# Picking the last tiles of every step by matmul, a third one in each fifth step, with the edge bias written into PSUM by ScalarE

## The chip, the core and the metric

The kernel runs on one core of a Trainium2 chip. The metric is the device time of one execution, in microseconds. An execution was also recorded by the hardware profiler; all instruction times below come from that record, and line numbers (L402) are lines of the kernel before.

## What is computed

A graph layer on 6250 nodes of 64 numbers and 206250 edges, sorted by destination. Of each edge, the key and value of its source node are needed, the query of its destination, and the edge's own projected features:

```
Qh, Kh, Vh = x @ Wq.T + bq, x @ Wk.T + bk, x @ Wv.T + bv     # (6250, 4 heads, 16)
Ee    = edge_attr @ We.T + be                                # (206250, 4, 16)
score = exp(clip((Kh[src] * Qh[dst] / 4 * Ee).sum(-1), -5, 5))
wV    = segment_sum(Vh[src] * score, dst)                    # (6250, 64)
out   = layernorm(x + wV)
```

## The kernel before

Edges are cut into 1612 tiles of 128, eight tiles to a group, and the loop at L708 goes through them in 105 steps: 97 of two groups (16 tiles) and 8 of one group at the end. What is written here is one branch of an If (L412); the other branch, a general method, is not taken by these inputs.

**Ahead of the loop.** Keys and values of all nodes are computed (L320, L322) and written to a table in HBM, kv_tab; the queries, split into three bf16 parts, to another, q3_tab. The kv of the first four groups are not taken from the table: GpSimd gathers rows of x (L230), and PE turns them and multiplies them by the weights (L370 to L384). GpSimd then gathers kv of groups 4 to 7 (L406).

**Keys and values of an edge (kv).** A ring of five buffers (KVB, L118) holds the kv of five steps, 16 tiles each. There are three ways into it. Nearly all tiles are gathered from kv_tab by one indirect DMA of GpSimd for each tile (gather_kv, L402). In every sixth step one tile comes row by row through SP's queue (fetch_rows, L528, and a copy, L548). And the last two tiles of most steps are "picked" by matmul: the nodes' x, in three bf16 parts, lies in SBUF as a table of 50 blocks of 128 rows (parts); VectorE compares the sources with the block numbers and makes a matrix of ones and zeros (hots, L481, in two halves of 25 blocks for each tile); 25 matmuls (a burst, L491) for each half pick the rows of x out of the table into PSUM; VectorE adds the three parts (picked, L498); PE turns the result (picked_turned, L505) and multiplies it by the weights (picked_kv, L513 and L515); ScalarE copies it into the ring (L516). A pick begun in step s delivers tiles 14 and 15 of step s + 2. In the kernel before, this is done in steps 4 to 94. The table is made in steps 0 to 3 by table_parts (L444): a load of x on SP's queue, copies by ScalarE and subtractions by VectorE.

**A step.** VectorE multiplies kv by the queries (products, L602) and by the edge values (L603), adds up each head (L609), clips it (L611); ScalarE takes Exp (L612); VectorE multiplies the values by it (message, L619). ScalarE and PE split the message into three bf16 parts (L622, and minus: L630, L632, twice). In the next step, 16 matmuls add up the messages by destination (sums, L638), and VectorE adds that to the open blocks of the output (add, L652). About every second step a block of 128 nodes is closed (close, L668, L677, L678); after 16, 32 and 47 closed blocks their norms follow, three in a step (norm, L688).

For the next step, while this one runs: PE spreads row numbers into PSUM (spread, L555), ScalarE makes of them a matrix of ones and zeros in two passes, Square (L572) and Relu (L577), PE multiplies the queries by it (queries, L595). PE also computes the next step's edge values in PSUM (edges, and edge_values L386): first a matmul that writes the bias (L388), then four f32 matmuls on top (L391), for each of the two groups.

**What sets the order.** The schedule is by hand: the order of the calls in the loop (L708 to L786) is the order in each engine's queue, and each engine goes through its queue in order. GpSimd's gathers of step s + 4 are called in step s, behind the message (L742); they write the ring buffer that step s - 1 has read. The PSUM tile pb is single, and spread and picked_turned take it in turn; so is pe, which the edge values of the next step overwrite when L603 has read them; and rows3, which the first burst of a step overwrites when L498 has read the picks of the step before. The tile small, also in PSUM, holds the turned sources, the scores and the sums side by side.

Of the kernel before, what the change touches and what calls it, by code (L numbers as in the profile page):

```python
# [14 lines left out]
P = 128  # L15
N = 6250
# [24 lines left out]
TB = 8  # L41
M0 = 4
# [21 lines left out]
LAST = NS - 8 - 3  # L64


def picks_in(s):
    return M0 <= s <= LAST

# [5 lines left out]
COLUMN = 2 * G - 3  # L75
# [27 lines left out]
def tile_gnn(ctx: ExitStack, tc: tile.TileContext, x, xT, wT, bias, beT, weT, eT, src, dst, dst_rows,  # L103
# [52 lines left out]
    bkv_p = consts.tile([3, G // 2, 2 * C], BF16, name="bkv_p")  # L156
    minus_b = consts.tile([P, P], BF16, name="minus_b")
# [26 lines left out]
    with tc.tile_pool(name="nodes", bufs=1) as nodes, \  # L184
# [36 lines left out]
        nc.sync.dma_start(be_sb, beT.to_broadcast([3, C]))  # L221
        nc.vector.memset(we_sb, 0.0)
# [147 lines left out]
        for g in range(XG):  # L370
            for h in range(2):
                tp = npsum.tile([P, 2, P], F32, name="tp", bufs=2)
                for u in range(2):
                    j = 4 * h + 2 * u
                    nc.tensor.transpose(tp[:, u, :],
                                        XS[g][:, j:j + 2, :].rearrange("p j c -> p (j c)"), ident)
                xe = nodes.tile([P, 2, P], F32, name="xe", bufs=2)
                nc.scalar.activation(xe, tp, AF.Copy)
                pv = npsum.tile([P, 4, 2 * C], F32, name="pv", bufs=2)
                nc.tensor.matmul(pv, ones_b, bkv_p, start=True, stop=False, skip_group_check=True)  # L380
                for u in range(2):
                    nc.tensor.matmul(pv[:, 2 * u:2 * u + 2, :], xe[:, u, :], wkv, start=False,
                                     stop=u == 1, skip_group_check=True)
                nc.scalar.activation(kv_of(g)[:, 4 * h:4 * h + 4, :], pv, AF.Copy)  # L384

    def edge_values(pe, et, n):  # L386

        nc.tensor.matmul(pe[:, :n, :], ones_b, be_p[:, :n, :], start=True, stop=False,  # L388
                         skip_group_check=True)
        for u in range(n // 2):  # L390
            nc.tensor.matmul(pe[:, 2 * u:2 * u + 2, :], et[:, u, :], we_sb, start=False,  # L391
                             stop=u == n // 2 - 1, skip_group_check=True)
# [13 lines left out]
    for g in range(XG, 2 * KVB - 2):  # L406
        for j in range(G):
            gather_kv(g, j)
# [3 lines left out]
    with tc.If(rv == 0) as branch:  # L412

        with tc.tile_pool(name="work", bufs=2) as work, \
# [5 lines left out]
            col, from0, from1 = (small[:, i * C:(i + 1) * C].bitcast(BF16) for i in range(3))  # L420
            from_b = from0, from1
            score_all = small[:, 3 * C:3 * C + 2 * G * H]
            pa = small[:, 4 * C:7 * C].rearrange("p (i c) -> p i c", i=3)
            nc.tensor.transpose(col, row_b[:, 0:1].to_broadcast([P, P]), ident_b)

            parts = accp.tile([P, NB, 3, C], BF16, name="parts")
            nc.vector.memset(parts, 0.0)
            NX = N // NB
            x_v = x.rearrange("(p b) c -> p b c", p=NX)
            n_picks = LAST - M0 + 1  # L430
            src_f = accp.tile([P, n_picks, 2], F32, name="src_f")
            t0 = (M0 + 3) * 2 * G - 2
            for i in range(2):
                nc.vector.tensor_copy(src_f[:, :, i],
                                      src_i[:, t0 + i:t0 + i + 2 * G * (n_picks - 1) + 1:2 * G])
            pick = fixed.tile([P, 4 * P], F32, name="pick")
            rows3 = pick[:, :6 * C].rearrange("p (k i c) -> p k i c", k=2, i=3)
            HOT, FAR, X = {}, {}, {}
# [5 lines left out]
            def table_parts(b):  # L444

                n = min(TB, NB - b)
                raw = work.tile([P, TB, C], F32, name="raw", bufs=1)
                nc.sync.dma_start(raw[:NX, :n], x_v[:, b:b + n, :])
                rest = pick[:NX, :n * C].rearrange("p (b c) -> p b c", b=n)
                nc.scalar.activation(rest, raw[:NX, :n], AF.Copy)  # L450
                nc.scalar.activation(parts[:NX, b:b + n, 0], raw[:NX, :n], AF.Copy)
                return rest

            def table_parts_rest(b, rest):
                n = min(TB, NB - b)
                nc.vector.tensor_sub(rest, rest, parts[:NX, b:b + n, 0])
                nc.scalar.activation(parts[:NX, b:b + n, 1], rest, AF.Copy)
                nc.vector.tensor_sub(parts[:NX, b:b + n, 2], rest, parts[:NX, b:b + n, 1])

            def sources(s, i):  # L460

                if picks_in(s):
                    FAR[s, i] = work.tile([P, P], BF16, name="far")
                    nc.scalar.activation(FAR[s, i], row50, AF.Identity,
                                         bias=src_f[:, s - M0, i:i + 1], scale=-1.0)

            def sources_turned(s, i):
                if picks_in(s):  # L470
                    nc.tensor.transpose(from_b[i], FAR.pop((s, i)), ident_b)  # L471
# [4 lines left out]
            def hots(s, i, h):  # L476

                if picks_in(s):
                    HOT[s, i, h] = work.tile([P, NB // 2, P], BF16, name="hot", bufs=4)
# [6 lines left out]
            def picks(s, i, h):  # L486
                if picks_in(s):
                    hot = HOT.pop((s, i, h))
                    for k in range(NB // 2):
                        b = h * NB // 2 + k  # L490
                        nc.tensor.matmul(rows3[:, i], hot[:, k, :], parts[:, b], start=b == 0,  # L491
                                         stop=b == NB - 1)

            def picked(s):

                if picks_in(s):
                    xp = work.tile([P, 2, C], F32, name="xp")
                    nc.vector.tensor_reduce(xp, rows3.rearrange("p k i c -> p k c i"), axis=AX.X,  # L498
                                            op=OP.add)
                    X[s] = xp  # L500

            def picked_turned(s):
                if picks_in(s):
                    room = psum.tile([P, G, P], F32, name="pb")
                    nc.tensor.transpose(room[:, 0, :], X[s].rearrange("p k c -> p (k c)"), ident)  # L505
                    xe = work.tile([P, P], F32, name="xe")
                    nc.scalar.activation(xe, room[:, 0, :], AF.Copy)
                    X[s] = xe, room[:, 4:6, :]

            def picked_kv(s):  # L510
                if picks_in(s):
                    xe, kv = X.pop(s)
                    nc.tensor.matmul(kv, ones_b, bkv_p[:, :2], start=True, stop=False,  # L513
                                     skip_group_check=True)
                    nc.tensor.matmul(kv, xe, wkv, start=False, stop=True, skip_group_check=True)  # L515
                    nc.scalar.activation(kvs[(s + 2) % KVB][:, 2 * G - 2:, :], kv, AF.Copy)  # L516

            def gather(s):
                for g in groups_of(s):
                    for j in range(tiles_of(g)):  # L520
                        if is_rowed(s) and (g - STEPS[s][0]) * G + j == COLUMN:
                            continue
                        if not picks_in(s - 2) or g == STEPS[s][0] or j < G - 2:
# [36 lines left out]
            def edges(s, k):  # L560

                g = STEPS[s][0] + k
                if k == 0:
                    PE[s] = psum.tile([P, 2 * G, C], F32, name="pe")
                edge_values(PE[s][:, k * G:(k + 1) * G], ET[g], tiles_of(g))
# [134 lines left out]
            closed, scaled, normed = 0, 0, 0  # L700
            keys(0)
# [5 lines left out]
            onehot_edges(0)  # L707
            for s in range(NS):  # L708
# [9 lines left out]
                if more:  # L718
                    onehot_rows(nexts[0], spread(nexts[0]))
                    onehot_rows_rest(nexts[0])  # L720
# [4 lines left out]
                if nexts[1:]:  # L725
                    onehot_rows(nexts[1], spread(nexts[1]))
                making = [b for b in range(s * 2 * TB, (s + 1) * 2 * TB, TB) if b < NB]
                if making:
                    rest = table_parts(making[0])
                prod = products(s)  # L730
                picked(s - 1)
                if more:
                    edges(s + 1, 0)
                picks(s, 0, 0)
                score = scores(s, prod)
                if nexts[1:]:
                    onehot_rows_rest(nexts[1])
# [5 lines left out]
                picked_turned(s - 1)  # L743
                if nexts[1:]:
                    edges(s + 1, 1)
                minus(s, msg, 0)
                hots(s, 1, 0)
                picks(s, 0, 1)
                minus(s, msg, 1)
                picked_kv(s - 1)  # L750
# [5 lines left out]
                picks(s, 1, 0)  # L756
                sources(s + 1, 1)
                sources(s + 2, 0)
                if s + 1 < NS:
                    rows_fetched(s + 1)  # L760
                if more:
# [5 lines left out]
                hots(s + 1, 0, 0)  # L767
                hots(s + 1, 0, 1)
# [14 lines left out]
                for i, b in enumerate(making):  # L783
                    if i:
                        rest = table_parts(b)
                    table_parts_rest(b, rest)  # L786
# [4 lines left out]
            scales(B - 2, B - 1)  # L791
            norm(B - 2)
            last_add(NS - 1)
            spreads(B - 1)
            roots(B - 1, B)
            scales(B - 1, B)
            norm(B - 1)

    with branch.Else():

        sums = [dram.tile([NR, C], F32, name=f"sums{i}") for i in range(TABLES)]
        with tc.tile_pool(name="gconsts", bufs=1) as gc, \
                tc.tile_pool(name="gloads", bufs=3) as loads, \
                tc.tile_pool(name="ggath", bufs=4) as gath, \
# [28 lines left out]
            def gather(g, j):  # L833
# [3 lines left out]
                if g >= 2 * KVB - 2:  # L837
# [11 lines left out]
            def compute(g):  # L849
# [33 lines left out]
                AGG[g] = work.tile([P, G, C], F32, name="agg", bufs=3)  # L883
# [79 lines left out]
```

## Time and profile before

| | |
|---|---|
| time, median of 3 runs | 1790.06 us (1789.95 to 1790.13) |
| the profiled execution's own time | 1789.88 us |
| its span, first to last instruction | 1788.0 us |
| PE, TensorE's matmuls, busy | 1638.5 us (92%) |
| PEld, its weight loads, busy | 1369.6 us (77%) |
| DVE, VectorE, busy | 1481.6 us (83%) |
| ACT, ScalarE, busy | 914.0 us (51%) |
| POOL, GpSimd, busy | 1337.4 us (75%) |
| matmuls that pick (L491) | 9100, 828.3 us |
| granted TensorE clock, mean | 0.951 |

A line of the groups gives the source line, engine, operation, what it writes and reads with shapes and how many, then the busy time and the mean of one in ns, then how long the engine was idle just before them and what ended that. In a timeline the first two columns are the start and the duration in us. Matmuls are pipelined, so a busy PE isn't PE at its peak. "Issue" is time in which an engine waited for nothing that the profile shows. A line of the windows gives the stretch, its length, then PE, PEld, DVE, ACT and POOL busy with their counts, the granted clock, the share of DMA and GB/s.

### The profile page before, as it was taken

The numbers are of one execution on the slowest core, as the hardware profiler recorded it, in microseconds if no ns is written. First come the engines' busy times: TensorE is split into PE (matmuls) and PEld (weight loads), VectorE is DVE, ScalarE is ACT, GpSimd is POOL, SyncE is SP. The second block draws the span as 40 slices with busy tenths as digits, with TensorE's granted clock in tenths as the row PEclk, the third lists the DMA queues.
The fourth block names the chain that finished last, engine by engine and source line by source line (L and its number), as shares of the span: only waits on it lengthen the run. The fifth ranks groups of instructions, "written<-read, shape, count | busy, mean of one in ns | idle before, by whom it ended". The sixth has DMA issues, their size and how long they took to land.

```text
span 1788.0 us, 44286 instructions
## 1 busy us (share of the span) xinstructions
PE 1638.5 (92%) x15751; PEld 1369.6 (77%) x15751; DVE 1481.6 (83%) x1695; ACT 914.0 (51%) x1328; POOL 1337.4 (75%) x1427
## 2 busy tenths in 40 slices
PE   8978999999999998999999899999989998999864
PEld 8647888888888787787887778777877887787632
DVE  6459999999998898888889888888988888898654
ACT  3465555555554464454455445455544554455443
POOL 7777777777777777777777777777777777777774
PEclk9968999999999999999999999999999999999855
DMA  7443333333333333332333333323332333333331
GB/s 221 132 121 84 90 93 94 93 94 92 93 81 94 93 86 89 92 94 80 93 93 81 93 81 93 92 81 99 87 93 80 94 93 81 93 90 81 91 80 44
DMA packets 109970, 166.71 MB, mean 93 GB/s; under 512 B 69196, under 2 KB 71452, under 8 KB 109626
## 3 DMA queue, kind: packets, MB, share of 16 engines
q0 software_dynamic: 45280, 91.78, 19.4%
q1 hardware_dynamic: 64074, 71.01, 14.1%
q8 instruction: 125, 2.05, 0.5%
q10 hardware_dynamic: 384, 1.00, 0.3%
q14 instruction: 107, 0.88, 0.2%
HBM read 156.33 MB, written 7.33 MB: 92 GB/s over the span
## 4 chain that ended last, share of the span: by engine, by line
PE 38%; POOL 29%; issue 14%; DVE 13%; DMA 4%; ACT 3%; DVEq 0%; SPq 0%; POOLq 0%; ACTq 0%
POOL kv L402 29%; PE pick L491 18%; PE pe L391 5%; DVE hot L481 5%; DMA kv<-kv_tab,src_i 3%; PE pq L630 2%; PE small L638 2%; DVE prod L603 2%; DVE prod L602 2%; PE pb L555 2%; PE pe L388 2%; PE pb L515 1%; PE pq L595 1%; DVE pq L619 1%; PE ps L350 1%
## 5 line engine op out<-in xcount | busy, mean ns | idle before, releaser
L402 POOL DMA_INDIRECT kv<-kv_tab,src_i x1383 | 1305.3, 944 | 421.7 <-issue 399.8
L491 PE MATMUL pick<-parts,hot 128*128 128x192 bf16 x9100 | 828.3, 249 | 0.0
L491 PEld LDWEIGHTS <-hot 128*128 128x128 bf16 x9100 | 771.7, 99 | 38.1
L481 DVE TENSOR_TENSOR hot<-small,block 128x3200 bf16<-128x3200 bf16 x364 | 645.3, 1813 | 0.4 <-PE pick L491 0.4
L572 ACT ACTIVATE to<-pb,minus_row 126x1024 bf16<-126x1024 f32 x202 | 222.7, 1102 | 371.0 <-PE pb L555 367.2
L632 ACT ACTIVATE msg<-pq 128x1024 bf16<-128x1024 f32 (+2 forms) x210 | 207.6, 989 | 222.3 <-PE pq L630 222.3
L391 PEld LDWEIGHTS pe<-we_sb,et 128*128 128x128 f32 x1612 | 209.7, 203 | 133.4 <-issue 95.3
L602 DVE TENSOR_TENSOR prod<-kv,pq 128x1024 f32<-128x1024 f32 (+2 forms) x105 | 123.5, 1176 | 169.3 <-DMA kv<-kv_tab,src_i 52.0
L391 PE MATMUL pe<-we_sb,et 128*128 128x128 f32 x1612 | 250.3, 302 | 0.0
L577 ACT ACTIVATE to<-to,one_p 126x1024 bf16<-126x1024 bf16 x202 | 230.6, 1142 | 3.5
L638 PEld LDWEIGHTS <-of 128*128 128x128 bf16 x1612 | 145.3, 102 | 31.1 <-issue 7.9
L638 PE MATMUL small<-msg,of 128*128 128x192 bf16 x1612 | 161.9, 257 | 0.5 <-ACT msg L632 0.5
L388 PE MATMUL pe<-be_p,ones_b 3*128 3x512 bf16 x202 | 79.7, 395 | 86.3 <-DVE prod L603 86.1
L630 PE MATMUL pq<-msg,minus_b 128*128 128x512 bf16 x404 | 128.0, 396 | 33.1 <-ACT msg L622 19.5
L622 ACT ACTIVATE msg<-pq 128x1024 bf16<-128x1024 f32 (+2 forms) x105 | 103.8, 989 | 96.8 <-DVE pq L619 96.8
L609 DVE TENSOR_REDUCE small<-prod 128x64 f32<-128x1024 f32 (+2 forms) x105 | 123.6, 1177 | 14.5 <-PE small L471 8.8
L555 PE MATMUL pb<-key_rows,ident_b 112*128 112x512 bf16 x403 | 127.9, 400 | 2.8 <-ACT to L572 2.8
L603 DVE TENSOR_TENSOR prod<-prod,pe 128x1024 f32<-128x1024 f32 (+2 forms) x105 | 123.6, 1177 | 3.6
L619 DVE TENSOR_TENSOR pq<-kv,small 128x1024 f32<-128x1024 f32 (+2 forms) x105 | 123.4, 1175 | 1.4 <-ACT small L612 1.4
L585 DVE TENSOR_TENSOR of<-small,key 128x2048 bf16<-128x2048 bf16 (+2 forms) x105 | 122.9, 1171 | 0.3
L595 PEld LDWEIGHTS <-to 126*128 126x128 bf16 x1612 | 63.5, 101 | 25.3 <-issue 25.1
L612 ACT ACTIVATE small<-small 128x64 f32<-128x64 f32 (+2 forms) x105 | 21.7, 207 | 111.1 <-DVE small L611 109.2
(129 smaller groups left out, 996.4 us busy)
## 6 DMA issues: line engine op xcount, KB each, us to landing
et<-in_eT SPq DMA_DIRECT2D x100, 512.0 KB
rk<-kv_tab SPq DMA_DIRECT2D x1920, 0.5 KB
kv<-kv_tab,src_i POOLq DMA_INDIRECT x1383
qw<-q_tab SPq DMA_DIRECT2D x202, 15.8 KB
kv_tab<-kv_sb SPq DMA_DIRECT2D x5, 640.0 KB
q_tab<-q SPq DMA_DIRECT2D x5, 480.0 KB
acc<-in_x SPq DMA_DIRECT2D x48, 32.0 KB
out<-y SPq DMA_DIRECT2D x48, 32.0 KB
```

Of the source, the lines that this page charges most:

```text
L391: nc.tensor.matmul(pe[:, 2 * u:2 * u + 2, :], et[:, u, :], we_sb, start=False, stop=u == n // 2 - 1, skip_group_check=True)
L402: nc.gpsimd.indirect_dma_start(out=kv_of(g)[:, j, :], out_offset=None, in_=kv_tab[:, :], in_offset=bass.IndirectOffsetOnAxis(ap=src_i[:, t ...
L481: nc.vector.tensor_tensor(HOT[s, i, h].rearrange("p b (a c) -> p b a c", c=2), pairs(from_b[i])[:, None].to_broadcast(shape), block2[:, bl ...
L491: nc.tensor.matmul(rows3[:, i], hot[:, k, :], parts[:, b], start=b == 0, stop=b == NB - 1)
L555: nc.tensor.matmul(pb[:, b:b + 4, :], ident_b[:NR2, g // 2:g // 2 + 1].to_broadcast([NR2, P]), key_rows[:, g % 2, b * P:(b + 4) * P], star ...
L572: nc.scalar.activation(TO[g][:, :n, :], pb[:3 * W, :n, :], AF.Square, bias=minus_row3[:3 * W])
L577: nc.scalar.activation(TO[g][:, :n, :], TO[g][:, :n, :], AF.Relu, bias=one_p[:3 * W], scale=-1.0)
L602: nc.vector.tensor_mul(prod[:, :n, :], kvs[s % KVB][:, :n, :C], PQ[s][:, :n, :])
L603: nc.vector.tensor_mul(prod[:, :n, :], prod[:, :n, :], PE[s][:, :n, :])
L630: nc.tensor.matmul(msg[:, lo:hi, :], minus_b, M3[s][:, lo:hi, i, :], start=False, stop=True, skip_group_check=True)
L632: nc.scalar.activation(M3[s][:, :n, i + 1, :], msg[:, :n, :], AF.Copy)
L638: nc.tensor.matmul(PA[s], OH[s][:, j, :], M3[s][:, j], start=j == 0, stop=j == n - 1)
```

## The change

- Steps 0 to 96 pick (before: 4 to 94), and every fifth step from 0 to 90 picks a third tile, tile 13 of step s + 2. The tile that comes row by row moves from 13 to 12. The third tile's hots, its two bursts (into the PSUM tile pb) and one more reduction stand at the end of the step and at the head of the next; its x is turned and multiplied apart (64 rows). There are five hot tiles and three far tiles instead of four and two.
- The table of parts is made ahead of the loop, from the transposed x that already lies in SBUF: 50 transposes on PE, copies by ScalarE, subtractions by VectorE, placed between the kv of the first four groups, whose turning now goes one half ahead. The seven loads in steps 0 to 3 go, and a load of the bias for all partitions joins SP's queue at the start.
- The edge bias of steps 1 to 104 is written into PSUM by one ScalarE copy for a step (biases), and the edge matmuls add to it. pe is a fixed tile. Step 0 keeps its two bias matmuls.
- In a step the sums come first on PE; the first spreading comes behind the sources, and on ScalarE its Square and Relu stand around Exp and the bias; the second spreading and the edges of both groups come behind the first burst, the message and the gathers' call.
- picked_turned goes from ahead of the first subtraction to behind the second burst, picked_kv from there to behind the third burst.
- At the very end, the last addition goes ahead of scales and norm of the block before the last.

```diff
+THIRD = 5
+TB = 4
-LAST = NS - 8 - 3
+LAST = NS - 8 - 1
+def picks_third(s):
+    return picks_in(s) and s % THIRD == 0 and STEPS[s + 2][1] == 2
...
+            px = npsum.tile([P, 2, 2 * C], F32, name="ps").rearrange("p i (j c) -> p (i j) c", j=2)
+            px = px[:, :n]
+            for u in range(n):
+                nc.tensor.transpose(px[:, u, :], xT_sb[:C, (b + u) * P:(b + u + 1) * P],
+                                    ident[:C, :C])
+            nc.scalar.activation(parts[:, b:b + n, 0], px, AF.Copy)
+            nc.vector.tensor_sub(px, px, parts[:, b:b + n, 0])
+            halves.append((px, b, n))
...
+    def edge_values(pe, et, n, biased=False):
+
+        if not biased:
+            nc.tensor.matmul(pe[:, :n, :], ones_b, be_p[:, :n, :], start=True, stop=False,
+                             skip_group_check=True)
...
+                    if i == 2 and h == 0:
+                        R3[s] = psum.tile([P, G, P], F32, name="pb")
...
+            def picked_third(s):
+
+                if picks_third(s):
+                    to = R3.pop(s).rearrange("p g e -> p (g e)")[:, :3 * C]
+                    nc.vector.tensor_reduce(X[s][:, 0], to.rearrange("p (i c) -> p c i", i=3),
+                                            axis=AX.X, op=OP.add)
...
+            def biases(s):
+                n = tiles_in(s)
+                nc.scalar.activation(pe_all[:, :n, :], be_all[:, None, :].to_broadcast([P, n, C]),
+                                     AF.Copy)
...
                 nexts = list(groups_of(s + 1)) if more else []
-                if more:
-                    onehot_rows(nexts[0], spread(nexts[0]))
-                    onehot_rows_rest(nexts[0])
                 if s:
                     sums(s - 1)
                 sources_turned(s, 1)
                 sources_turned(s + 1, 0)
-                if nexts[1:]:
-                    onehot_rows(nexts[1], spread(nexts[1]))
-                making = [b for b in range(s * 2 * TB, (s + 1) * 2 * TB, TB) if b < NB]
-                if making:
-                    rest = table_parts(making[0])
+                sources_turned(s, 2)
                 prod = products(s)
                 picked(s - 1)
+                picked_third(s - 1)
                 if more:
-                    edges(s + 1, 0)
+                    onehot_rows(nexts[0], spread(nexts[0]))
                 picks(s, 0, 0)
                 score = scores(s, prod)
-                if nexts[1:]:
-                    onehot_rows_rest(nexts[1])
+                if more:
+                    biases(s + 1)
+                    onehot_rows_rest(nexts[0])
                 if s:
                     add(s - 1)
                 msg = message(s, score)
                 if s + KVB - 1 < NS:
                     gather(s + KVB - 1)
-                picked_turned(s - 1)
                 if nexts[1:]:
-                    edges(s + 1, 1)
+                    onehot_rows(nexts[1], spread(nexts[1]))
+                for k in range(len(nexts)):
+                    edges(s + 1, k)
                 minus(s, msg, 0)
+                if nexts[1:]:
+                    onehot_rows_rest(nexts[1])
                 hots(s, 1, 0)
                 picks(s, 0, 1)
+                picked_turned(s - 1)
                 minus(s, msg, 1)
-                picked_kv(s - 1)
...
                 hots(s, 1, 1)
                 picks(s, 1, 0)
+                picked_kv(s - 1)
                 sources(s + 1, 1)
                 sources(s + 2, 0)
+                sources(s + 1, 2)
...
                 picks(s, 1, 1)
-                hots(s + 1, 0, 0)
-                hots(s + 1, 0, 1)
+                for h in range(2):
+                    hots(s, 2, h)
+                for h in range(2):
+                    picks(s, 2, h)
+                for h in range(2):
+                    hots(s + 1, 0, h)
...
             sums(NS - 1)
             roots(B - 2, B - 1)
             close(B - 1)
-            scales(B - 2, B - 1)
-            norm(B - 2)
             last_add(NS - 1)
             spreads(B - 1)
             roots(B - 1, B)
+            scales(B - 2, B - 1)
+            norm(B - 2)
```

## The prediction

> **What bounds the kernel now.** First the page's groups, for the engine that is never let go: of GpSimd's idle time before gathers nearly all is "issue", its own 0.30 us between two of them.
>
> ```profile
> span 1788.0 us, 44286 instructions
> L402 POOL DMA_INDIRECT kv<-kv_tab,src_i x1383 | 1305.3, 944 | 421.7 <-issue 399.8
> L481 DVE TENSOR_TENSOR hot<-small,block 128x3200 bf16<-128x3200 bf16 x364 | 645.3, 1813 | 0.4 <-PE pick L491 0.4
> ```
>
> Then the timeline of POOL at both ends:
>
> ```profile
> 2.80 1.10 POOL L230 DMA_INDIRECT xs<-in_x,src_x  x1 [0.54 <-DMA src_x<-in_src]
> ...
> 1768.85 0.94 POOL L402 DMA_INDIRECT kv<-kv_tab,src_i  x1 [0.30 <-issue]
> ```
>
> From 2.80 to 1769.79 there are 32 + 1383 = 1415 gathers, 1.248 us each, without a hole. The last 18.2 us (1788.0 - 1769.8) are what the last group still does. So GpSimd's queue sets the end. Next, how far the compute is behind it. The windows and the waits say that there are two regimes:
>
> ```profile
> 150.00:375.00 225.00, 225.00 (x2357) 193.25 (x2356) 211.87 (x219) 123.92 (x174) 170.09 (x181) 1.00 0.34 91
> 1200.00:1690.00 490.00, 452.79 (x4607) 385.00 (x4607) 416.93 (x442) 246.65 (x344) 370.24 (x393) 0.98 0.33 89
> ```
> ```profile
> DVE prod L602 <- DMA kv<-kv_tab,src_i: 52.0, 34, 4.0
> ```
>
> The first two columns after the window are its length and PE's busy time. From 150 to 375 us PE is busy for all of it: there the compute runs at its own pace, on tiles that were gathered up to four steps early. By step (products L602 against the end of that step's last gather) this lead shrinks from 54 us at step 2 to 2 us at step 28, and from then on VectorE waits for gathers and PE is 92% busy. The compute's own pace is in the chain of waits of a window of the first regime, all PE, and VectorE's timeline beside it:
>
> ```profile
> 208.75 0.43 PE pb L555 x2
> ...
> 224.49 0.43 PE pb L555 x2
> 224.92 1.32 PE small L638 x16
> 226.25 0.11 PE small L471 x2
> 226.36 0.43 PE pb L555 x2
> 226.79 0.32 PE pe L388
> 227.11 1.09 PE pe L391 x8
> 228.20 2.06 PE pick L491 x25
> ```
> ```profile
> 206.86 0.58 DVE L668 TENSOR_REDUCE y<-acc 128x64 f32<-128x256 f32 x1
> ...
> 208.36 1.22 DVE L602 TENSOR_TENSOR prod<-kv,pq 128x1024 f32<-128x1024 f32 x1 [0.29 <-issue]
> ...
> 210.75 0.55 DVE L498 TENSOR_REDUCE xp<-pick 128x128 f32<-128x384 f32 x1
> ...
> 222.83 1.21 DVE L602 TENSOR_TENSOR prod<-kv,pq 128x1024 f32<-128x1024 f32 x1
> ```
>
> One step is 15.74 us of PE (208.75 to 224.49). VectorE's step is 14.47 us (208.36 to 222.83), and 1.5 us more when a block is closed (206.86 to 208.36).
>
> **Gathers removed.** Steps 0 to 96 pick two tiles each (194), and 19 of them (0, 5, ... 90) a third: 213 instead of 182. GpSimd has 1352 gathers of kv left, 31 fewer: 31 x 1.248 = 38.7 us. If its queue never stopped, it would end at 2.8 + 1384 x 1.248 = 1730 us. The question is who is late next.
>
> **PE.** In an ordinary step the two bias matmuls go (2 x 0.32): 15.74 - 0.64 = 15.10 us. A third tile costs 50 matmuls at 2.06/25 us = 4.12, its turning of sources 0.06, and in the next step the turning of x, its kv matmul and a longer bias row, 0.11 + 0.32 + 0.10: 4.71 together, 19 times in 97 steps: 0.92 a step. 16.02 us a step, if PE never waits.
>
> **VectorE.** 62 hots more: 3.47 us in a third step and a reduction of about 0.35 after it. 14.47 + 49/97 x 1.5 for the closes + 0.75 = 16.0 us a step. Two engines that hand work to each other at 16.0 us each can't both be full.
>
> **The order, where I expect the loss.** Sums are now PE's first work in a step, then the sources, the first spreading, and then the first burst of picks; the second spreading and the edges, 0.43 + 1.41 us, that stood ahead of that burst come behind it. The burst overwrites what L498 reduces, so PE is held there, with the rest of its step queued behind, and ScalarE and VectorE wait for that in turn. Before the change PE had 0.43 + 1.32 + 0.11 + 0.43 + 1.41 = 3.7 us of work up to it, now 1.86. L498 ends 2.95 us after the products start (208.36 to 211.30). After an ordinary step the products start 1.66 us ahead of PE's step (222.83 against 224.49): L498 ends at +1.3, before +1.86, nothing is lost. After a close they start about 0.4 us ahead (208.36 against 208.75): L498 ends at +2.6, PE waits 0.7, and with the later Exp and the bias behind it about 0.8. The next step starts fresh. 49 closes in 97 steps: 0.40 a step. After a third step PE is late itself (4.7 against 3.8 us) and the close costs nothing there, but the next spreading, and the first burst behind it, wait until VectorE has read the third tile out of the same PSUM: about 0.7 again when a block is closed, so I keep 0.40 for all. The norms, three to a step in some 16 steps, add about 0.05. Sum: 16.02 + 0.45 = 16.47 us a step.
>
> **ScalarE's bias.** 104 writes of 128x1024 into PSUM: L632, the same size out of PSUM, takes 1.02 us and L577 1.14 us; below, it would be nothing beyond what it replaces. I take 1.02. It stands after Exp and ahead of L577 and the message's copy L622. ScalarE has some 9 us of a step's 15.7 busy (123.92 of 225 us), so it has the room; on PE the edges wait for it, with the first subtraction from the message and the second burst queued behind them. Counted from PE's start in an ordinary step: Exp ends at +3.4, bias +4.35, PE gets to the edges at +4.35; the copy ends at +6.35, PE gets to it at +6.5. Cost nothing by a hair; if the first burst, which is that cover, were shorter, up to 1.0 a step. The turning of picked x one burst later and its kv product stay inside PE's sum and give ScalarE's copy a whole burst (2.06 us) of cover. The kv tiles are needed one step later still: nothing.
>
> **The start.** The parts of x are no longer made in steps 0 to 3 (seven loads leave SP's queue there, one bias load joins it at the top) but ahead of the loop, with 50 transposes on PE. There PE is full between 53 and 77 us (23.3 of 24) and slow: the eight kv halves take 3.03 us each, and a 65x128 weight load with its 64 columns took 0.216 us (18.15 us for 84, L350). 50 x 0.22 = 11 us later, if that pace holds. The Trainium skill speaks to whether it does (TensorE: Matmul & The Clock Gate, section PE-mode transpose): transposes don't count as work for the clock gate. By it PE stays slow, 11 us; were the denser work to warm it, the two f32 matmuls of a half would take about 1.3 us (0.63 each in the loop, L515) instead of the 2.07 seen, a gain of 7 us over eight halves, and transposes half: 2 us earlier. I take the 11. Step 0 then picks a third tile at a slow start, about 3.5 us. Products of step 0: 85 + 11 + 0.5 = 96.5 us, and 3.5 in that step.
>
> This also holds up GpSimd: step 5's gathers need the buffer of step 0, read by its message, 6.5 us after the products. GpSimd, with five gathers fewer by then, is there at 2.8 + 73 x 1.248 = 94 us, and waits for 103; then for step 1's message, some 5 us: about 14 us in all. Its queue would end at 1744, the kernel at 1762.
>
> **A rule against the change.** 62 more hots are 112 us of VectorE. By the Trainium skill (SBUF — State Buffer, section SBUF: two separate sides) a VectorE operation that takes both SBUF ports locks GpSimd out of writing descriptors: up to 112 us of gathers stopped. The row: 1.248 us a gather through 645 us of hots, whose one operand lies in PSUM. I take nothing.
>
> **Sum.** 96.5 + 3.5 + 97 x 16.47 = 1697.6 at the products of step 97. To step 104's products in the trace of before: 1774.05 - 1708.91 = 65.1, held by GpSimd in part; at the 9 us that its unheld half steps took, six of them and the 7.4 of the last: 62. The end is 1788.0 - 1774.05 = 13.95 behind that; there the last addition goes ahead of the scale, the norm and the store (SP) of the block before, worth 0.5 us at most, not counted. 1773.6, plus the 1.88 that the profiled run has around its span (1789.88): 1775.5. Ten closes fall to third steps at 0.7 and not 0.8, and that last half microsecond may come: 1774. The profiled run of before stands 0.2 us under the median of 1790.06, so no correction.
>
> **Rivals.** (1) GpSimd remains the bound: PE and VectorE share the waits better and stay below 16.35 a step. Then 1730 + 18.2 + 1.9 = 1750 without the stall at the start, 1764 with it. For it: the ring of five buffers that evens out third steps; against: 16.02 on both engines. (2) Slower: the first burst waits for L498 in every step, not after closes alone, because VectorE no longer gets its 1.66 us ahead (its own reduction of scores waits for PE's sums and sources). Price 0.8 in each step: 15.10 + 0.92 + 0.8 + 0.05 = 16.87 a step, 177.8 + 97 x 16.87 = 1814 us. It decides from 16.62 a step on (177.8 + 97 x 16.62 = 1790). For it: 14.47 + 1.5 is over 15.10, VectorE is the slower one in half the steps; against: in the trace the lead comes back within one step.
>
> **Numbers.** Pair of PE and VectorE binds, 1767 to 1786: 0.46; GpSimd binds, 1750 to 1766: 0.24; slower, 1794 to 1820: 0.21; in between, 1786.5 to 1793.5: 0.09. Within 0.2% (about what a measurement can tell) lies only the last. Faster 0.70, same 0.09, slower 0.21. The range 1754 to 1806 leaves out the ends of (1) and (2).
>
> **What would show it.** Gathers 1352; the period of PE's chain after 150 us: 15.1 in ordinary steps, 15.9 after a close, 19.3 in a third step, with PE's waits named L549 (the reduction's new line); GpSimd waiting for the message at about 94 us; VectorE over 90% busy. Wrong if PE's bursts wait elsewhere (the edges for the bias), if POOL's gathers grow beyond 1.25 us, or if steps wait for gathers again before step 90.

## The result, and the profile after

The changed kernel took 1760.05 us (median of 4 runs, 1758.92 to 1760.39), the kernel before 1790.01 us beside it (1789.95 to 1790.13): a ratio of 0.9831, 95% interval 0.9816 to 0.9847. The profiled execution took 1759.85 us, with a span of 1758.1 us. Eight of the runs below fell on chips (numbered 1, 7, 10, 11 and 15 in the record) where the kernel before took 3075 to 3095 us beside them; in the step shown below PE stands still there while gathers are in flight, and times from there are compared only with each other.

GpSimd first. The page's group, and the timeline of POOL at its first stop and at its end (the bracket is the idle time before, and what ended it):

```profile
L449 POOL DMA_INDIRECT kv<-kv_tab,src_i x1352 | 1276.0, 944 | 415.9 <-issue 389.3
```
```profile
96.92 0.94 POOL L449 DMA_INDIRECT kv<-kv_tab,src_i  x1 [2.80 <-DVE pq L684]
...
1733.84 0.94 POOL L449 DMA_INDIRECT kv<-kv_tab,src_i  x1 [0.30 <-issue]
```

A gather still takes 944 ns and 0.30 us to the next. The queue stops twice at the start (here, and 1.61 us ahead of the gather at 115.71), for 4 us beyond the usual 0.30, and ends at 1734.8 us, 35 us earlier than before; the kernel ends 23.3 us after it, not 18.2. So the gathers removed are there in full, and GpSimd's own floor, with the tail and the 1.9 us around the span that the kernel before had, is 1734.8 + 18.2 + 1.9 = 1755 us, an estimate from these sums. The windows (length, PE, PEld, DVE, ACT, POOL) show that PE is nearly full, and not in the first steps alone (219.46 of the 225 us from 150 to 375):

```profile
1200.00:1660.00 460.00, 442.90 (x4785) 392.44 (x4783) 433.02 (x452) 267.66 (x380) 347.66 (x369) 1.00 0.34 91
```

Of the waits of the whole span:

```profile
PE pick L535 <- DVE xp L549: 33.0, 38, 2.3
...
PE pe L438 <- ACT pe L629: 14.4, 8, 3.2
...
PE pb L615 <- DVE xp L542: 9.8, 10, 1.4
...
DVE prod L667 <- DMA kv<-kv_tab,src_i: 6.5, 17, 1.5
```

VectorE's wait for gathers has fallen from 52.0 to 6.5 us, and most of that is no wait for a gather: 14 of the 17 are 0.29 us each, and all but those of steps 89, 91 and 96 stand where the step's gathers had ended at least 7 us before. Step 96 alone waits longer than 0.7 us, 1.47. Set against the end of each step's last gather, the products (L667) are 64.6 us late at step 2, 44 us at step 20, and only from step 89 to 96 between 1.7 and 5.4 us. Compute runs at its own pace, (1680.70 - 108.08) / 96 = 16.38 us a step from the products of step 1 to those of step 97, while GpSimd needs about 17.0 us for a step's gathers; compute catches up with it just where the picking ends.

### The profile page after: what moved, and what is told of

Same layout as the page of the kernel before. It is cut to its first block, busy times and chain, and to the rows that moved or that the text cites. A ratio compares the mean times of both kernels' runs of the same rounds, so it can differ in the third digit from the quotient of the medians.

```text
span 1758.1 us, 47673 instructions
## 1 busy us (share of the span) xinstructions
PE 1669.0 (95%) x17263; PEld 1463.4 (83%) x17263; DVE 1593.8 (91%) x1796; ACT 1006.3 (57%) x1499; POOL 1308.2 (74%) x1396
## 4 chain that ended last, share of the span: by engine, by line
PE 36%; DVE 24%; POOL 21%; issue 11%; ACT 4%; DMA 3%; DVEq 0%; SPq 0%; ACTq 0%; POOLq 0%
POOL kv L449 21%; PE pick L535 16%; DVE hot L521 11%; PE pe L438 5%; DVE prod L668 3%; DVE prod L667 3%; DMA kv<-kv_tab,src_i 3%; PE small L703 3%; PE pq L695 3%; PE pb L615 2%; ACT to L637 2%; DVE of L650 1%; PE pb L535 1%; PE pb L571 1%; PE pq L660 1%
## 5 line engine op out<-in xcount | busy, mean ns | idle before, releaser
L449 POOL DMA_INDIRECT kv<-kv_tab,src_i x1352 | 1276.0, 944 | 415.9 <-issue 389.3
L535 PEld LDWEIGHTS <-hot 128*128 128x128 bf16 x10650 | 884.7, 98 | 111.7 <-issue 47.5
L535 PE MATMUL pick<-parts,hot 128*128 128x192 bf16 x9700 | 865.4, 246 | 35.1 <-DVE xp L549 33.0
L521 DVE TENSOR_TENSOR hot<-small,block 128x3200 bf16<-128x3200 bf16 x426 | 753.5, 1813 | 0.0
L438 PEld LDWEIGHTS pe<-we_sb,et 128*128 128x128 f32 x1612 | 194.8, 197 | 55.3 <-ACT pe L629 51.7
L438 PE MATMUL pe<-we_sb,et 128*128 128x128 f32 x1612 | 213.9, 287 | 14.4 <-ACT pe L629 14.4
L667 DVE TENSOR_TENSOR prod<-kv,pq 128x1024 f32<-128x1024 f32 (+2 forms) x105 | 123.2, 1173 | 50.0 <-PE pq L660 17.9
L703 PE MATMUL small<-msg,of 128*128 128x192 bf16 x1612 | 155.0, 251 | 0.5 <-ACT msg L697 0.5
L576 ACT ACTIVATE kv<-pb 128x256 f32<-128x256 f32 (+1 forms) x97 | 39.2, 404 | 190.2 <-PE pb L571 135.3
L703 PEld LDWEIGHTS <-of 128*128 128x128 bf16 x1612 | 137.7, 100 | 1.9 <-issue 1.5
L629 ACT ACTIVATE pe<-be_all 128x1024 f32<-128x1024 f32 (+1 forms) x104 | 102.4, 984 | 0.0
```

What stands on the lines that cost most here:

```text
L449: nc.gpsimd.indirect_dma_start(out=kv_of(g)[:, j, :], out_offset=None, in_=kv_tab[:, :], in_offset=bass.IndirectOffsetOnAxis(ap=src_i[:, t ...
L521: nc.vector.tensor_tensor(HOT[s, i, h].rearrange("p b (a c) -> p b a c", c=2), pairs(from_b[i])[:, None].to_broadcast(shape), block2[:, bl ...
L535: nc.tensor.matmul(to, hot[:, k, :], parts[:, b], start=b == 0, stop=b == NB - 1)
L667: nc.vector.tensor_mul(prod[:, :n, :], kvs[s % KVB][:, :n, :C], PQ[s][:, :n, :])
L703: nc.tensor.matmul(PA[s], OH[s][:, j, :], M3[s][:, j], start=j == 0, stop=j == n - 1)
```

## Experiments

Paces below are taken between the products of steps 20 and 80, which hold 12 thirds. The changed kernel has (1401.99 - 415.68) / 60 = 16.44 us a step there.

**Gathers left out, 35 of them.** Ahead of the test in gather:

```
+                        if s % 5 in (1, 3) and 10 < s < 97 and g == STEPS[s][0] and j == 0:
+                            continue
```

> The changed kernel, but 35 gathers of kv (first tile of two steps in five, from step 11 to 96) are left out, so those tiles hold the kv of an earlier step; all compute stays. 35 x 1.248 = 43.7 us of GpSimd's queue. Theory A, PE and VectorE set the pace from step 2 to 96 and the gathers only touch in the last steps (VectorE waited 6.5 us in all for them): 1753 to 1760 us. Theory B, GpSimd's queue is the bound: 1716 us, or as far down as the compute lets it. It is also the control of the next kernels, since GpSimd can't hide there what the compute gains.

Measured: 3093.1 us, the kernel before 3094.4 (ratio 0.9989, 0.9977 to 1.0). No answer to the question, as everything is late on that chip. Twice more, with the same kernel, on two other chips:

> The control again (35 gathers left out, all compute kept), since in its first run the kernel before took 3094 us and not 1790, on a chip where PE stood still between its matmuls. Where the kernel before takes 1790 us: theory A, PE and VectorE set the pace: 1753 to 1760 us. Theory B, GpSimd's queue is the bound: 1716 us or little more.

3090.9 us against 3094.9 (0.9986, 0.9976 to 0.9996).

> The control once more (35 gathers left out, all compute kept), as the first two runs fell where the kernel before takes 3094 us. Where the kernel before takes 1790 us: theory A, PE and VectorE set the pace: 1753 to 1760 us. Theory B, GpSimd's queue is the bound: 1716 us or little more.

3051.0 us against 3074.9 (0.9916, 0.9892 to 0.994).

**A third in every fourth step.** `-THIRD = 5`, `+THIRD = 4`.

> A third tile in every fourth step, 24 instead of 19. GpSimd has 5 gathers fewer, 6.2 us. Theory A: five thirds more at 4.71 us of PE each, 23.5 us less the 6.5 us that steps wait for gathers now: 1777 to 1784 us. Theory B: 1754 us.

3147.0 us (1.0167 of before, 1.0153 to 1.0181). Neither theory's number could come out where the kernel before takes 3094 us.

**Bias by matmul, and the reduction first, each with those 35 gathers left out.** The edits are shown further down, where they were run again without any gathers.

> The changed kernel with 35 gathers left out (as in the control), and the bias put in by two bf16 matmuls a step as before the change; ScalarE's bias goes. PE gets 2 x 0.32 us a step more. If ScalarE's bias was hidden, as the prediction took it: 0.64 x 96 = 61 us over the control, about 1817 us. Rival: PE waited 51.7 + 14.4 us for that bias in all, so the two forms cost PE the same: within 8 us of the control, about 1756 us.

3138.3 us, 45 us over the control.

> The changed kernel with 35 gathers left out (as in the control), and VectorE reduces the picks of the step before ahead of the products and not behind them, 2.4 us earlier, so that the first burst never waits for it. If that wait costs its recorded 33 us: up to 33 us below the control, about 1723 us. Rival: the products, and with them Exp, ScalarE's bias and the edges, come 0.55 us later in each step, and PE waits there instead: no gain, or up to 15 us slower than the control.

3174.0 us, 81 us over the control. Both have the sign that the later runs confirm.

**The changed kernel on a chip of that kind.** No edit.

> The changed kernel as it is, beside the kernel before. Where the kernel before takes 1790 us: 1760 us again. Where it takes some 3090 us, as beside the last runs, PE stands still between its matmuls for about 1000 us and GpSimd has time to spare, so the gathers removed are worth nothing. Theory A and B agree there: the time is that of the control with 35 gathers left out, 3050 to 3095 us, and the gain over the kernel before is under 1%. If instead it is 30 us or more above the control, gathers cost something even there.

3129.1 us against 3093.5: 1.0115 (1.0085 to 1.0144), slower than the kernel before, and 36 us over the control, which ran on other chips. The expectation "under 1% gain, at the control's time" fell; gathers do cost something there. The timeline of PE in one step shows where:

```profile
1024.92 0.42 PE L660 MATMUL pq<-qw,to 126*128 126x64 bf16 x5 [1.14 <-issue]
1025.15 4.19 PE L535 MATMUL pick<-parts,hot 128*128 128x192 bf16 x25
```

Most of the 16 small query matmuls come in ones and twos, over 1 us apart; "issue" is a wait for nothing that the profile shows. GpSimd's gathers of this step go out between 1004.9 and 1022.1 us, and their last packets move at 1023. Up to 1011.2 us PE still ran at nearly its usual speed (a burst at 1008.77 took 2.40 us). The burst behind the stop takes 4.19 us, the next one 2.23 as usual. That led to the next kernel.

**All gathers of steps 8 to 96 left out.**

```
+                        if 8 <= s < 97:
+                            continue
```

> The changed kernel with all gathers of kv for steps 8 to 96 left out (those tiles keep the kv of an earlier step); all compute stays, so the pace from step 12 to 96 is the compute's own. Theory A, PE and VectorE set the pace of the changed kernel at 16.37 us a step where it took 1760 us: the pace stays at 16.2 to 16.4 us a step. Theory B, GpSimd's queue held it: 16.0 us a step (PE's busy time) or less. Where the kernel before takes 3090 us there is a third question: PE stands still there in the second half of each step's gathers. If the gathers in flight are what holds it, the stops vanish with them and the pace falls from 29 to about 16 us a step; if it is TensorE's own limit, the pace stays near 29 us.

1877.3 us, where the kernel before took 3094.0. The stops are gone with the gathers, so it isn't a limit of TensorE by itself. From step 20 to 80, (1496.07 - 519.13) / 60 = 16.28 us a step. The windows of exactly these 60 steps, here and in the changed kernel where it took 1760 us:

```profile
519.00:1496.00 977.00, 958.21 (x10372) 849.40 (x10370) 934.68 (x979) 578.96 (x820) 0.00 (x0) 1.00 0.14 39
```
```profile
416.00:1402.00 986.00, 958.25 (x10367) 849.17 (x10365) 936.93 (x979) 578.58 (x820) 745.15 (x791) 1.00 0.34 91
```

PE and VectorE do the same work in the same time, at a granted clock of 1.00, and with no gather at all they gain only 9 us in 60 steps. By pace that is theory A: not GpSimd but PE (98% busy) and VectorE (96%) set the changed kernel's pace. Theory B wanted 16.0 or less. Even the 9 us aren't GpSimd's queue: 8.7 of them lie in the 29 steps with a close, most of which are 0.35 to 0.39 us shorter without gathers. There the products come behind the close's short instructions, and VectorE first goes through its instructions that wait for the gathers, though these had ended long before. The views of the products in such a step (562.5 to 563.2 us in the changed kernel, 664.4 to 665.1 here):

```profile
L667 DVEq EVENT_SEMAPHORE  x5: 21/50/50, 562.6 to 563.0; - x5
```
```profile
L669 DVEq EVENT_SEMAPHORE  x1: 21/21/21, 664.9 to 664.9; - x1
```

In a step without a close, where at least one compare of 1.81 us stands before the products, nothing is gained but in two of 31. And this kernel is a control in which GpSimd can hide nothing. The four that follow have its edit too; they ran where the kernel before took 1790.2 us, so the totals in their expectations, which start from 1877.3 us, don't apply, and paces are compared. (That the control's pace carries over is seen in single steps: mostly 14.45 us an ordinary step and 15.99 with a close, in the control and in the kernel without thirds alike.)

**Bias by matmul.**

```
-                edge_values(PE[s][:, k * G:(k + 1) * G], ET[g], tiles_of(g), s > 0)
+                edge_values(PE[s][:, k * G:(k + 1) * G], ET[g], tiles_of(g))
...
-                    biases(s + 1)
```

> All gathers of steps 8 to 96 left out, as in the control no_gathers (1877.3 us, 16.24 us a step from step 20 to 60), and the bias put in by two bf16 matmuls a step as before the change; ScalarE's bias goes. If ScalarE's bias was hidden, as the prediction took it: 2 x 0.32 us a step more, 16.9 us a step, 97 x 0.64 = 62 us over the control: 1939 us. Rival: PE waits about as long for ScalarE's bias as the matmuls took (51.7 + 14.4 us in the changed kernel's trace): within 8 us of the control.

1782.95 us; (1426.41 - 420.36) / 60 = 16.77 us a step, 0.49 over the control.

```profile
420.00:1426.00 1006.00, 999.65 (x10490) 864.18 (x10488) 938.31 (x979) 537.03 (x761) 0.00 (x0) 1.00 0.14 38
```

PE's work grows by (999.65 - 958.21) / 60 = 0.69 us a step, and its idle time falls from 18.8 to 6.4 us, 0.21 a step. So ScalarE's bias is worth 0.49 us a step, some 47 us in 97 steps, and the rival, that it only trades work for a wait, is wrong. That it is not the whole 0.69 isn't a wait for the bias. The waits of the control's 60 steps, then one of this kernel's:

```profile
PEld pe L438 <- ACT pe L631: 20.9, 59, 0.4
...
PE pick L535 <- DVE xp L549: 15.4, 20, 2.4
```
```profile
PE pick L535 <- DVE xp L549: 6.2, 5, 2.4
```

Only weight loads wait for the bias there, 0.35 us each, while PE still has earlier matmuls to do; no matmul does. With more work of its own PE waits less for VectorE's reduction. It is otherwise in the seven half steps, which pick nothing: 13.5 of the 14.4 us that matmuls wait for the bias in the changed kernel are there, and these steps take 64.3 us there, 64.1 and 64.2 in the last two kernels below, and 61.1 with the bias by matmul.

**The reduction ahead of the products.**

```
-                prod = products(s)
                 picked(s - 1)
+                prod = products(s)
```

> All gathers of steps 8 to 96 left out, as in the control (1877.3 us), and VectorE reduces the picks of the step before ahead of the products and not behind them, 2.4 us earlier, so that the first burst doesn't wait for that behind the products. If that wait is a loss by itself: up to 25 us below the control, 1852 us. Rival: the products, Exp, ScalarE's bias and the edges come 0.55 us later in each step, and later still where the last burst ends late, as VectorE then waits for PE ahead of its products: 0 to 60 us over the control.

1836.6 us; (1470.39 - 433.31) / 60 = 17.28 us a step, 1.00 over the control, more than even the rival allowed. Its waits in the 60 steps:

```profile
PE pe L438 <- ACT pe L631: 72.1, 48, 2.9
DVE xp L549 <- PE pick L535: 61.0, 44, 3.2
```

VectorE now waits 1 us a step for PE's last burst before it may start the products. Behind them come scores, Exp and ScalarE's bias, and there PE waits in turn. The first burst's wait is gone and a longer one is in its place: the products are the head of the step's chain, and must not wait for PE.

**The close later.** The loop of closes goes from the end of a step to behind the next step's message:

```
                 msg = message(s, score)
+                while closed < B - 2 and due[closed] < s:
+                    close(closed)
+                    spreads(closed)
+                    closed += 1
...
-                    while closed < B - 2 and due[closed] <= s:
-                        close(closed)
-                        spreads(closed)
-                        closed += 1
```

> All gathers of steps 8 to 96 left out, as in the control (1877.3 us), and the close of a block stands behind the next step's message and not at the end of its own step. The prediction's term: a close puts the products back by 1.5 us and PE then waits 0.8 us at the first burst, 49 times, 0.40 us a step. If so, PE's waits for L549 and L542 are nearly gone and the time is 25 to 39 us below the control: 1838 to 1852 us. Rival: VectorE is the one that is full, and the 1.5 us only go elsewhere in its queue, ahead of the hots, where the second tile's bursts wait for them: within 5 us of the control.

1735.3 us; (1385.64 - 408.93) / 60 = 16.28 us a step: the control's pace to the hundredth. PE's waits for the two reductions of picks over the same 60 steps:

```profile
PE pick L535 <- DVE xp L549: 12.9, 19, 2.1
...
PE pb L617 <- DVE xp L542: 5.8, 6, 1.9
```

Together they are 18.7 us here and 15.4 + 3.1 = 18.5 in the control, though no close stands ahead of the products any more. The rival is right: VectorE has its 1.5 us to do somewhere, and between these two places nothing is lost or won.

**No thirds but the first.** `-THIRD = 5`, `+THIRD = 1000`.

> All gathers of steps 8 to 96 left out, as in the control (1877.3 us), and only step 0 picks a third tile, so 18 thirds go (their tiles aren't picked and keep old kv). By the prediction's price, 4.71 us of PE each: 85 us below the control, 1792 us, and PE stays the full engine. Rival: VectorE, with 3.82 us for each, is what is full: 69 us below, 1808 us. A loss smaller than 60 us would mean that a third fills holes that are there anyway.

1659.0 us; (1323.22 - 399.87) / 60 = 15.39 us a step, 0.89 less.

```profile
400.00:1323.00 923.00, 901.60 (x9719) 794.59 (x9717) 888.88 (x941) 571.97 (x796) 0.00 (x0) 1.00 0.15 41
```

Twelve thirds cost (976.9 - 923.3) / 12 = 4.47 us each, and PE's work alone falls by (958.21 - 901.60) / 12 = 4.72. So hardly anything of a third lies in holes, 0.25 us by these two numbers. The steps without one run 14.45 us, and 15.99 with a close: that is VectorE's own 14.47, and 1.5 for the close, as the timeline of before had them. PE's work, 901.60 / 60 = 15.03 us a step, lies in between.

## Why the prediction was right, and where its size was off

It said 1774 us and a gain of 16; it was 1760 and a gain of 30. The side holds, and by pace the likeliest case does: the pair of PE and VectorE takes over, GpSimd's queue is no longer what each step waits for. By its number alone the result would have told the other way: 1760 lies in the range given to GpSimd as the bound (1750 to 1766) and not in that of the pair (1767 to 1786), and only the paces and the run without gathers tell the two apart. How the 15.5 us between its sum (1775.4) and the profiled 1759.85 arise: -8.4 up to the products of step 1 (108.08, not 116.5), -8.5 from 96 steps at 16.38 and not 16.47, +2.3 in the half steps (1745.01 - 1680.70 = 64.3), -0.85 in the tail (1758.1 - 1745.0 = 13.1), and -0.1 around the span.

**The start is the term that was mis-sized.** "50 x 0.22 = 11 us" was priced from one record of the f32 matmuls of L350, which have two each (100 records for 50 matmuls). The timeline of PE in one half of the preamble after, and of two transposes of before:

```profile
55.69 1.11 PE L409 MATMUL ps<-ident,xT_sb 64*128 64x64 f32 x8
56.73 0.60 PE L396 MATMUL pv<-bkv_p,ones_b 3*128 3x512 bf16 x1
57.27 2.08 PE L398 MATMUL pv<-wkv,xe 128*128 128x256 f32 x4
59.14 0.64 PE L388 MATMUL tp<-ident,xs 128*128 128x128 f32 x2
```
```profile
54.88 0.64 PE L375 MATMUL tp<-ident,xs 128*128 128x128 f32 x2
55.45 0.60 PE L380 MATMUL pv<-bkv_p,ones_b 3*128 3x512 bf16 x1
```

Eight transposes hold up the next matmul by 56.73 - 55.69 = 1.04 us, 0.13 each and not 0.22, and a half, counted from its first line of L388 at 55.12 to the next at 59.14, takes 4.02 us where it took 3.03. The trace of before had a row of their kind: two transposes with twice the columns hold up the next matmul by 55.45 - 54.88 = 0.57 us, and half of one, 0.14, would have been a near estimate. The products of step 0 start at 91.08, 6.1 us later than before and not 11.5. The Trainium skill could have warned of that row: a transpose skips the arithmetic of a matmul (Perfetto Trace Analysis, section Transposes); that section gives no price. The other half of the argument held: the 50 transposes didn't make PE faster, the kv matmuls beside them still take 2.08 us (TensorE: Matmul & The Clock Gate, section PE-mode transpose, agrees). That a gated clock is why they are slow isn't shown: the granted clock in the windows is 1.00 there, before and after. The "3.5 us more in step 0" were 108.08 - 91.08 - 16.38 = 0.6. With that, GpSimd's stall was 4 us, not 14: its queue was there at 94.1 as predicted, but the message ended at 96.65, not at 103.

**The pace** was right. PE's work: 16.02 predicted, 958.25 / 60 = 15.97 measured. Its waits: 0.45 predicted, (986.3 - 958.25) / 60 = 0.47. A third: 4.71 against 4.47 to 4.72. The waits also stand where the prediction put them: 44 of PE's 48 waits for the two reductions (33.0 us for L549, 9.8 for L542) are in the step behind a close, and 28 of them last 0.81 to 0.91 us, against 0.8. What fails is the reason, "the order, where I expect the loss". With the close moved behind the message the waits add up to the same and so does the pace: it isn't where the close stands that makes PE wait, but that VectorE's step with a close is longer than PE's work. The ordinary steps follow VectorE's sum (14.45, and 15.99 with a close), not PE's 15.1 and 15.9. Only behind a third does PE seem to be the late one: such a step takes mostly 15.48 us without a close, 1.03 more than an ordinary one, of which the reduction of the third (L542) is 0.35. ScalarE's bias, "nothing by a hair", did cost nothing in the full steps; in the half steps, where the first burst that covers it is missing, it cost some 3 us (64.3 against 61.1), about the 2.3 by which they were put too short.

**GpSimd as the bound** (the first rival) is wrong by pace: without any gather the steps are 1% faster, and that lies in VectorE's waiting instructions. But its floor of 1755 us is only 5 us below the time; had compute been faster, little more would have come. And at the very end gathers do count: from step 80 to 97 the changed kernel takes 278.7 us, the one with the close later and no gathers 270.7. **Slower**, with the burst waiting in every step, would have needed 16.62 us a step. The rule on VectorE shutting GpSimd out, taken at nothing, cost nothing: with 62 hots more a gather takes 944 ns as before. The point at which steps would wait for gathers again was put behind step 90; they come within 2.7 us of it at step 89, and wait in earnest at step 96 alone.

What stays open is what holds the engines on the other chips: it was found only so far that it goes with the gathers.

## What to carry to other kernels

Once an engine's queue is relieved, read the pace from the stretch where the steps run free of it, and test it by leaving the queue's work out: that told in one run what the partial removals here, on chips where everything is late, had not. Price an added instruction from a row of the same kind, a transpose from a transpose. And before a wait is put down to an order, ask whether the engine waited for is full: if it is, moving its work only moves the wait.

## What was not expected of the hardware

On five chips the same kernels took 1.7 to 1.8 times as long, 3129 us against 1760 for the changed one, with nearly the same duration of VectorE's instructions (hots 1.82 against 1.81 us). PE stood still in part of each step while gathers went out, at a granted clock of 0.77 from step 20 to 80, and with the gathers left out the pace over these steps fell from 30.4 us a step to 16.3, the clock 1.00. There the change made the kernel 1.2% slower: in the step shown GpSimd had waited 12.2 us for the message before its first gather, which fits a queue with time to spare, whose relief is worth nothing. Why the change costs time there stays open.

In the changed kernel five waiting instructions of VectorE, whose gathers had long ended, took about 0.37 us of most steps with a close, where only short instructions stood before them.
